# Two scan networks, two attention blocks and one ScalarE: dt as ln(1 + exp(x)), with the function tables loaded by the kernel

## The chip, the cores and the metric

The kernel runs on one NeuronCore of a Trainium2 chip. The metric is the device time of one execution in microseconds; a single run's time is that of this core. Five kinds of work run beside one another: TensorE matmuls (PE in the profile, its weight loads PEld), VectorE (DVE), ScalarE (ACT), GpSimd (POOL), and transfers that SyncE (SP) issues. Each engine runs its own instructions in program order and waits on semaphores for the others.

## The reference, cut to what matters

Four images of 56 x 56 tokens with 96 channels pass through four layers: a selective-scan block (L0), a second one with convolutions (L1), and two attention blocks with quantized feed-forward parts (L2, L3). Most of the work is in the selective scans. L0 and L1 each scan every image in four directions; this is one of them in L0:

```python
def selective_ssm(dtw, dtb, xw, A_log, D, seq):
    xz = jnp.einsum('bld,kd->blk', seq, xw)
    dt_raw = xz[..., :DT_RANK]
    b_ssm = xz[..., DT_RANK:DT_RANK + D_STATE]
    c_ssm = xz[..., DT_RANK + D_STATE:]
    dt = jax.nn.softplus(jnp.einsum('blr,dr->bld', dt_raw, dtw) + dtb)
    a = -jnp.exp(A_log)
    d_a = jnp.exp(dt[..., None] * a)
    d_b = dt[..., None] * b_ssm[:, :, None, :]
    def step(h, inp):
        da_t, db_t, x_t, c_t = inp
        h = da_t * h + db_t * x_t[..., None]
        y_t = jnp.einsum('bds,bs->bd', h, c_t)
        return (h, y_t)
    # ... jax.lax.scan over the 3136 tokens; 192 channels d, 16 states s
```

The step size dt is a softplus, ln(1 + exp(x)); the decay of each state is an exp of it. Around the scans the reference has a silu (of the gate z in L0 and L1, and after a convolution in L1) and a gelu (in the feed-forward part of L0). Those functions, and exp, run on ScalarE, which holds one set of function tables at a time.

## The kernel before: the parts that the change touches

A direction of an image is cut into 7 chunks of 448 tokens. A chunk is 8 rounds r = 0 to 7: two channel halves e times four groups q of states, with three scans (g = 0, 1, 2) a round. 2 layers x 4 images x 4 directions x 7 chunks make 224 chunks and 1792 rounds. While the rounds of one chunk run, the next chunk is prepared in pieces, one a round (the comments are added here):

```python
def step_size(self, ch, e, ps):                      # L476
    rows = slice(32, 32 + RANK[ch.l])
    self.nc.tensor.matmul(ps[:C], ch.par.wt[rows, C * e : C * e + C], ch.cf[rows], start=True, stop=True)
    return ps[:C]

def step_size_ahead(self, ch):                       # in round 1: half 1 into a "ps" bank, if one is free
    if self.held < BANKS:
        ch.pd.append(self.step_size(ch, 1, self.ps()[:, :CS]))

def softplus(self, ch):                              # in round 2: both halves
    for e in range(NE):
        if e == len(ch.pd):
            ch.pd.append(self.step_size(ch, e, self.pp()))
        dt = self.sp.tile([C, CS], F32, name="dtc")
        self.nc.scalar.activation(dt, ch.pd[e], AF.Softplus, bias=ch.par.dtb[:, e : e + 1])   # L492
        ch.dtc.append(dt)

def prepare(self, ch, follow, r):
    # ... r == 0: rows(follow), the projection from PSUM to SBUF
    elif r == 1:
        self.step_sizes(follow)                      # half 0 into the "pp" bank
        self.split(follow, 0)
    elif r == 2:
        self.softplus(follow)
        self.split(follow, 1)
    elif r == 3:
        self.times_u(follow, 0)                      # POOL: dt * u, L498
        for e in range(NE):
            self.park(follow.dtd, follow.dtc[e])     # to DRAM
    elif r == 4:
        self.times_u(follow, 1)
        # ... park and spread
```

The rounds themselves, and where work of the other layers is put between them:

```python
for n, (ch, e, q) in enumerate(rounds):
    # ...
    b, v, ahead = nxt
    for g in range(2 if ahead else 3):               # DVE, L659: v = du * b, b in PSUM
        nc.vector.tensor_tensor(v[:, g, TOKENS], ch.du[e][:, g], b, ALU.mult)
    self.prepare(ch, nexts.get(ch), r)
    self.half_round()
    self.spend((0.6, 0, 3.8, 0, 0, 0, 0, 0)[r], (0, 1.3, 0, 0, 0, 0, 1.3, 1.3)[r] + 1.3 * (r % NQ == 2))
    self.limit = ACT_LIMIT if r >= SOFTPLUS else 0.5 + 0.95 * 2 * (SOFTPLUS - r)
    yield "C", n, r                                  # slot C: steps of the other layers
    if more:
        nxt = begin(n + 1)                           # PE, L569: the next round's b
    if len(late) == 2:
        ended = late.pop(0)
        self.add_up(*ended)                          # PE: sums of the round two before, into y
    self.prepare_ahead(afters.get(ch), r)
    for g in range(NG):
        if g == 2:
            # ... keep_sums: ACT L721, Y <- y, after a round with q == 3
            yield "F", n, r                          # slot F: steps of the other layers
            if r == 1 and ch in nexts:
                self.step_size_ahead(nexts[ch])
        nc.vector.tensor_tensor_scan(v[:, g, way], da[g][:, way], v[:, g, way], 0.0, ALU.mult, ALU.add)  # L684
        # ... carry, then decay(n + 1, g): ACT L631, da = exp(na * dt), one of three
    nc.gpsimd.tensor_tensor(hc, v[:, :, TOKENS], ...)   # POOL L694: times C

def add_up(self, ch, e, q, hc):
    # ...
    for _ in range(int(max(0.0, WARM - self.work) / FILL + 0.5)):
        nc.tensor.matmul(self.y[:C], self.zeros, self.some, start=False, stop=False)   # L710, adds zeros
    # ... four matmuls of hc into y, L714
```

The steps of the other layers ("lanes": loading and the first projection, the middle with gelu, the convolution, the fusion, the attention) are generators. A step is started when its ScalarE and TensorE time fit into a running backlog (`room`, limits ACT_LIMIT 4.3 and PE_LIMIT 6.0) and when it holds no more than two "ps" banks with the others, one of which is lent away in rounds 0 and 1:

```python
held = sum(h[2] for h in self.live) - g[2] + new
fits = held <= self.banks - self.lend or new <= g[2] and held <= self.banks
if place[0] == self.slot and fits and self.room(act, pe):
    ...
```

Silu and gelu stand in such steps, as in the first projection:

```python
nc.scalar.activation(t[0], ps[0], AF.Silu, bias=b[:, 1:2])                  # L794
nc.scalar.activation(t[1][64:], ps[1][64:], AF.Silu, bias=b[64:, 2:3])
yield "F0 a.6"
```

No line of this kernel loads tables: the compiler puts a table load in front of an activation whose function the loaded set lacks. After the last scan the lanes that are left run alone, with more buffers (`late`).

Of the kernel before, what the change touches and what calls it, by code (L numbers as in the profile page):

```python
# [42 lines left out]
ACT_LIMIT, PE_LIMIT = 4.3, 6.0  # L43
SOFTPLUS = 2
BANKS, LATE_BANKS = 2, 4
# [5 lines left out]
ORDER = (((0, 0), (0, 1), (1, 0), (1, 1)), ((0, 1), (1, 0), (1, 1), (0, 0)))  # L51
WD = NE * 128 + NE * C + NE + NE * NQ * NG


# [109 lines left out]
class Net:  # L164
    def __init__(self, ctx, tc, aps, at, out):
        self.tc, self.nc, self.aps, self.at, self.out = tc, tc.nc, aps, at, out
        pool = lambda name, **kw: ctx.enter_context(tc.tile_pool(name=name, **kw))
        self.const = pool("const", bufs=1)
        self.big = pool("big", bufs=1)
        self.psum = pool("psum", bufs=1, space=bass.MemoryType.PSUM)  # L170
        self.dram = pool("dram", bufs=1, space=bass.MemoryType.DRAM)
        self.nw, self.depth, self.banks, self.ring = NW, DEPTH, BANKS, None
        self.setup()
        self.dg = None
        self.kept = (0, 0, 0)
        self.ready = set()
        self.held, self.lend, self.live, self.g = 0, 0, [], {}
        self.backlog, self.limit, self.paced = [0.0, 0.0], ACT_LIMIT, False
        self.work = 0.0
        self.U = [self.big.tile([C, L], F32, name=f"U{e}") for e in range(NE)]  # L180
        self.Y = [self.big.tile([C, L], F32, name=f"Y{e}") for e in range(NE)]
        self.wp = pool("work", bufs=2)
        self.scan_pool = ExitStack()
        self.sp = self.scan_pool.enter_context(tc.tile_pool(name="scan", bufs=2))
        self.pool = pool
        d = lambda name, *shape: [self.dram.tile(list(shape), F32, name=f"{name}{i}") for i in range(NB)]
        self.xd, self.xrd = d("x", C, L), d("xr", C, L)
        self.ud, self.zd, self.yd, self.md = d("u", DI, L), d("z", DI, L), d("y", DI, L), d("m", DI, L)

    def late(self):  # L190

        self.scan_pool.close()
        self.wp = self.pool("late", bufs=2)
        self.nw, self.depth, self.banks = LATE_NW, LATE_DEPTH, LATE_BANKS
        tags = (("ps", BANKS), ("da0", 1), ("da1", 1), ("da2", 1), ("pp", 1), ("b", 1), ("y", 1))
        self.ring = cycle([t for t in tags for _ in range(t[1])])
# [284 lines left out]

    def step_size_ahead(self, ch):

        if self.held < BANKS:
            ch.pd.append(self.step_size(ch, 1, self.ps()[:, :CS]))

    def softplus(self, ch):
        for e in range(NE):
            if e == len(ch.pd):
                ch.pd.append(self.step_size(ch, e, self.pp()))  # L490
            dt = self.sp.tile([C, CS], F32, name="dtc")
            self.nc.scalar.activation(dt, ch.pd[e], AF.Softplus, bias=ch.par.dtb[:, e : e + 1])  # L492
            ch.dtc.append(dt)

# [31 lines left out]
    def prepare(self, ch, follow, r):  # L526

        if r == 0:
            self.spread(ch.du, ch.dud[1], "du")
            self.spread(ch.dt, ch.dtd[1], "dt")  # L530
            self.fetch(ch, 3)
        if follow is None:
            return
        if r == 0:
            self.rows(follow)
        elif r == 1:
            self.step_sizes(follow)
# [46 lines left out]
    def scans(self):  # L584
# [23 lines left out]
        first, second = chunks[:2]  # L608
        self.held = 0
        self.parameters(first)  # L610
# [3 lines left out]
        for r in range(8):  # L614
            self.prepare(Step(), first, r) if r else self.rows(first)
        self.parameters(second)
        self.project_step(second, 0)
# [29 lines left out]

        nxt = begin(0)
        for g in range(NG):
            decay(0, g)  # L650
        late = []
        for n, (ch, e, q) in enumerate(rounds):
# [8 lines left out]
            self.half_round()  # L661
            self.spend((0.6, 0, 3.8, 0, 0, 0, 0, 0)[r], (0, 1.3, 0, 0, 0, 0, 1.3, 1.3)[r] + 1.3 * (r % NQ == 2))
            self.limit = ACT_LIMIT if r >= SOFTPLUS else 0.5 + 0.95 * 2 * (SOFTPLUS - r)
            yield "C", n, r
# [14 lines left out]
                    if r < SOFTPLUS:  # L679
                        self.limit -= 0.95  # L680
# [3 lines left out]
                nc.vector.tensor_tensor_scan(  # L684
# [16 lines left out]
    def add_up(self, ch, e, q, hc):  # L701

        nc = self.nc
        if q == 0:
# [77 lines left out]
    def project(self, l, i, xr, s):  # L782
# [11 lines left out]
        nc.scalar.activation(t[0], ps[0], AF.Silu, bias=b[:, 1:2])  # L794
        nc.scalar.activation(t[1][64:], ps[1][64:], AF.Silu, bias=b[64:, 2:3])
        yield "F0 a.6"
        nc.scalar.activation(t[1][:64], ps[1][:64], AF.Identity, bias=b[:64, 2:3])
# [50 lines left out]
    def window(self, d, rows, c):  # L848

        lo, hi = max(0, CR * c - 1), min(HS, CR * c + CR + 1)  # L850
        t = self.wp.tile([128, CR + 2, HS], F32, name="win", bufs=NWIN)[:rows]
        self.nc.sync.dma_start(
# [4 lines left out]
    def overlap(self, part, n, depth=9, ready=lambda c: True):  # L857
# [5 lines left out]
        while live or c < n:  # L863
# [4 lines left out]
            for g in list(live):  # L868
# [12 lines left out]
            self.held = sum(h[2] for h in self.live)  # L881
            yield
# [39 lines left out]
    def middle(self, i):  # L922
# [5 lines left out]
        def part(c):  # L928
# [18 lines left out]
            g.append(self.w())  # L947
            nc.scalar.activation(g[0], ps[0], AF.Gelu, bias=self.b1[:, :1])
            yield "C2 p2.6"
            for m in (1, 2):  # L950
# [3 lines left out]
            for m in (1, 2):  # L954
                g.append(self.w())
                nc.scalar.activation(g[m], ps[m], AF.Gelu, bias=self.b1[:, m : m + 1])
            yield "C1 p3.9"
            ps = self.ps()[:C, :CW]
# [14 lines left out]
        def convolve(c):  # L973
# [8 lines left out]
            t = self.w()  # L982
            nc.scalar.activation(t, ps, AF.Silu, bias=par("c128", "1conv_ba"))
            yield "C1 p2.2"
            ps = self.ps()
# [5 lines left out]
            for h in range(2):  # L991
                nc.scalar.activation(
                    t[:, h * CW // 2 : (h + 1) * CW // 2], o[h], AF.Silu, bias=par("c128", "1conv_bb")[:64]
                )
            yield "C0"
            nc.sync.dma_start(self.ud[i][128:, s], t)
# [234 lines left out]
def tile_net(ctx: ExitStack, tc: tile.TileContext, aps, at, out):  # L1231
# [5 lines left out]
    def alone(lanes):  # L1237
        net.slot, net.lend, net.paced = "C", 0, False
        while lanes:
# [10 lines left out]
    E = mybir.EngineType  # L1250
    with tc.manual_schedule(engines={E.PE, E.Activation, E.DVE, E.Pool}):
        lanes = []
        for slot, n, r in net.scans():
            p, u = divmod(n, rounds)
            net.slot, net.lend, net.paced = slot, int(r < 2), True
            if slot == "C" and u == 2 and p < 8:
# [29 lines left out]
```

## Time and profile before

| | us |
|---|---|
| time, median of 3 runs | 9209.74 (9199.88 to 9211.36) |
| profiled execution, span | 9209.2 |
| before the first scan | 111.4 |
| from the first scan to the end of the last | 8724.9 |
| after the last scan | 372.9 |
| DVE busy | 7881.9 (86%) |
| POOL busy | 7838.3 (85%) |
| PE busy | 7868.1 (85%) |
| ACT busy | 6148.3 (67%) |

"Busy" is the time in which an engine has at least one instruction running. In the list of groups a row gives line, engine, operation and tiles, the count behind an x, then after the bar the busy time of the group and the mean duration of one in ns, and after the second bar the idle time of that engine just before the group's instructions, with what ended it. In a view of waits each row is who waited <- for whom: us in total, times, longest us. In a timeline a row is start, duration, engine, line, operation, out<-in; the bracket tells how long the engine had been idle before it and what ended that.

### The profile page before, as it was taken

How to read it: one execution, taken by the hardware profiler on the slowest of the kernel's cores; microseconds unless marked ns; L12 is line 12 of the kernel's file. 1: busy time of each engine (PE TensorE's matmuls, PEld its weight loads, DVE VectorE, ACT ScalarE, POOL GpSimd, SP SyncE). 2: the span in 40 equal slices, each digit the busy share in tenths (PEclk: the TensorE clock that was granted, in tenths of full speed). 3: DMA queues.
4: the chain of work that ended last, by engine and by line, in shares of the span. 5: the costliest groups of instructions: out<-in, count | busy, mean ns of one | idle time of the engine just before them, and what ended most of it. 6: DMA issues, size and time to landing. Idle time of an engine off the chain costs nothing. (4 is left out here: it accounts for less than half of the span.)

```text
span 9209.2 us, 124390 instructions
## 1 busy us (share of the span) xinstructions
PE 7868.1 (85%) x35426; PEld 3036.5 (33%) x35426; DVE 7881.9 (86%) x10198; ACT 6148.3 (67%) x12259; POOL 7838.3 (85%) x4320
## 2 busy tenths in 40 slices
PE   7888888898888888988889888887888888987897
PEld 3333333333333333333333333333333333333344
DVE  5999999899998999989988997899888898888941
ACT  5777677676777677766776655577656776566645
POOL 5998989989898989889888997899888998888941
PEclk9899989989899988999888998888888888887986
DMA  5776676667666676767666775566755567655721
GB/s 151 176 179 169 166 171 164 157 153 177 162 168 157 157 181 161 169 150 177 162 148 152 168 170 136 136 153 160 171 138 143 141 164 172 147 138 134 168 77 39
DMA packets 951352, 1418.11 MB, mean 154 GB/s; under 512 B 176578, under 2 KB 943812, under 8 KB 949796
## 3 DMA queue, kind: packets, MB, share of 16 engines
q1 hardware_dynamic: 949888, 1408.37, 63.5%
q8 instruction: 278, 4.55, 0.2%
q14 instruction: 414, 3.39, 0.1%
q10 hardware_dynamic: 772, 1.80, 0.1%
HBM read 1141.42 MB, written 268.14 MB: 153 GB/s over the span
## 5 line engine op out<-in xcount | busy, mean ns | idle before, releaser
L684 DVE TENSOR_TENSOR_SCAN v<-da,v 128x449 f32<-128x449 f32 (+1 forms) x5376 | 5484.4, 1072 | 244.6 <-ACT da L631 111.0
L694 POOL TENSOR_TENSOR hc<-v,cb 128x1344 f32<-128x1344 f32 x1792 | 5168.0, 2885 | 573.5 <-DVE v L684 257.2
L631 ACT ACTIVATE da<-dt,na 128x448 f32<-128x448 f32 x5376 | 3392.8, 635 | 1690.3 <-DVE v L684 1650.9
L659 DVE TENSOR_TENSOR v<-du,b 128x448 f32<-128x448 f32 x4172 | 2342.3, 609 | 663.0 <-PE b L569 532.4
L714 PE MATMUL y<-hc,four 128*32 128x448 f32 x14336 | 1913.8, 609 | 0.0
L710 PE MATMUL y<-w,zeros 128*96 128x448 bf16 x7084 | 1716.6, 380 | 0.0
L639 POOL TENSOR_TENSOR v<-du,cb 128x448 f32<-128x448 f32 x1204 | 1373.7, 1141 | 79.0 <-DMA cb<-cd 41.6
L710 PEld LDWEIGHTS <-zeros 128*96 128x96 bf16 x7084 | 918.5, 130 | 1049.4 <-issue 639.9
L569 PE MATMUL b<-cf,sel 128*128 128x448 bf16 x1792 | 708.3, 395 | 350.9 <-DVE v L659 350.1
L761 POOL TENSOR_TENSOR rs<-rs,power 112x4 f32<-112x4 f32 x252 | 254.2, 1010 | 546.9 <-ACT rs L760 361.6
L427 PE MATMUL pp<-U,wd 96*128 96x448 f32 x896 | 674.5, 840 | 14.3 <-DMA U<-u 14.3
L721 ACT COPY Y<-y 96x448 f32<-96x448 f32 x448 | 341.3, 762 | 468.8 <-PE y L714 468.4
L841 PE MATMUL ps<-win,dg 64*64 64x220 f32 (+10 forms) x1962 | 568.4, 491 | 55.3 <-ACT dtc L492 47.0
L714 PEld LDWEIGHTS y<-hc,four 128*32 128x32 f32 x14336 | 295.3, 113 | 951.0 <-issue 649.1
L498 POOL TENSOR_TENSOR duc<-dtc,U 96x448 f32<-96x448 f32 x448 | 559.6, 1249 | 2.5 <-ACT dtc L492 2.5
L708 PE MATMUL y<-Y,ident 96*96 96x448 f32 x672 | 543.4, 898 | 11.4 <-ACT carry L688 8.9
L631 ACT ACT_TABLE_LOAD x385 | 494.0, 1283 | 15.1 <-DMA dt<-dd 8.3
L582 POOL TENSOR_TENSOR cf<-cf 64x448 f32<-64x448 f32 x448 | 417.7, 932 | 38.1 <-ACT cf L466 3.0
L569 PEld LDWEIGHTS <-sel 128*128 128x128 bf16 x1792 | 195.4, 109 | 741.4 <-issue 737.9
L688 ACT COPY carry<-v 128x3 f32<-128x3 f32 x1536 | 295.7, 193 | 172.1 <-DVE v L684 169.6
L765 PE MATMUL ps<-ident,rs 112*96 112x112 f32 x1752 | 267.7, 308 | 158.3 <-POOL rs L761 87.7
L841 PEld LDWEIGHTS ps<-win,dg 64*64 64x64 f32 (+2 forms) x1962 | 236.8, 169 | 423.7 <-issue 317.2
(414 smaller groups left out, 6457.5 us busy)
## 6 DMA issues: line engine op xcount, KB each, us to landing
cb<-cd SPq DMA_DIRECT2D x3584, 112.0 KB, 4.1
dt<-dd SPq DMA_DIRECT2D x1792, 168.0 KB, 4.4
du<-dd SPq DMA_DIRECT2D x1792, 168.0 KB, 4.2
dd<-dtc SPq DMA_DIRECT2D x448, 168.0 KB, 2.0
dd<-duc SPq DMA_DIRECT2D x448, 168.0 KB, 2.0
U<-u SPq DMA_DIRECT2D x112, 168.0 KB, 4.5
z<-w SPq DMA_DIRECT2D x56, 224.0 KB, 3.8
u<-w SPq DMA_DIRECT2D x56, 224.0 KB, 3.2
```

Of the source, the lines that this page charges most:

```text
L427: self.nc.tensor.matmul(ch.ps.rearrange("p (a b) -> p a b", b=HS), ch.par.wx[:, e], self.in_order(self.U[e], ch.orient, ch.c * CS, CS), st ...
L498: self.nc.gpsimd.tensor_tensor(du.rearrange("p (a b) -> p a b", b=HS), ch.dtc[e].rearrange("p (a b) -> p a b", b=HS), self.in_order(self.U ...
L569: self.nc.tensor.matmul(ps, self.sel[:, q], self.upper(ch.cf), start=True, stop=True)
L631: nc.scalar.activation(da[g][:, TOKENS], ch.dt[e][:, g], AF.Exp, scale=ch.par.na[:, e, q, g : g + 1])
L639: nc.gpsimd.tensor_tensor(v[:, 2, TOKENS], ch.du[e][:, 2], ch.cb[q][:, 1], ALU.mult)
L659: nc.vector.tensor_tensor(v[:, g, TOKENS], ch.du[e][:, g], b, ALU.mult)
L684: nc.vector.tensor_tensor_scan(v[:, g, way], da[g][:, way], v[:, g, way], 0.0, ALU.mult, ALU.add)
L694: nc.gpsimd.tensor_tensor(hc, v[:, :, TOKENS], ch.cb[q][:, 0].unsqueeze(1).to_broadcast([128, NG, CS]), ALU.mult)
L708: nc.tensor.matmul(o, w, self.in_order(a, ch.orient, ch.c * CS, CS), start=True, stop=False)
L710: nc.tensor.matmul(self.y[:C], self.zeros, self.some, start=False, stop=False)
L714: nc.tensor.matmul(self.y[32 * n : 32 * n + 32], self.four, hc[:, g], start=n == 3, stop=n == 3 or q == NQ - 1,)
L841: self.nc.tensor.matmul(o[:, a - r0 : e - r0, x0:x1], diag[:, tap], win[:, a + dy - lo : e + dy - lo, x0 + dx : x1 + dx], start=n == 0, st ...
```

## The change

dt is computed as ln(1 + exp(x)) by two activations, Exp and then Ln with a bias of 1, in place of one Softplus. One set of tables holds both exp and ln (set 6). The kernel loads it itself: once in front of the scans, and again behind every silu and gelu, so that neither the decays nor dt need another set. dt of half 0 is made in round 2 and of half 1 in round 3. With that go the devices that made room for the old round 2: the lent bank, the lower ScalarE limit in rounds 0 and 1, the second projection ahead into a "ps" bank (it now goes into "pp" in round 2). Two smaller things go along: no filler matmuls ahead of the sums that end a half (q == 3), and more window buffers after the last scan.

```diff
+EXP_AND_LN = 6
...
-        self.nw, self.depth, self.banks = LATE_NW, LATE_DEPTH, LATE_BANKS
+        self.nw, self.nwin, self.depth, self.banks = LATE_NW, LATE_DEPTH, LATE_DEPTH, LATE_BANKS
...
-    def step_size_ahead(self, ch):
-
-        if self.held < BANKS:
-            ch.pd.append(self.step_size(ch, 1, self.ps()[:, :CS]))
-
-    def softplus(self, ch):
-        for e in range(NE):
-            if e == len(ch.pd):
-                ch.pd.append(self.step_size(ch, e, self.pp()))
-            dt = self.sp.tile([C, CS], F32, name="dtc")
-            self.nc.scalar.activation(dt, ch.pd[e], AF.Softplus, bias=ch.par.dtb[:, e : e + 1])
-            ch.dtc.append(dt)
+    def softplus(self, ch, e):
+        dt = self.sp.tile([C, CS], F32, name="dtc")
+        self.nc.scalar.activation(dt, ch.pd[e], AF.Exp, bias=ch.par.dtb[:, e : e + 1])
+        self.nc.scalar.activation(dt, dt, AF.Ln, bias=1.0)
+        ch.dtc.append(dt)
...
         elif r == 2:
-            self.softplus(follow)
+            self.softplus(follow, 0)
             self.split(follow, 1)
         elif r == 3:
+            self.softplus(follow, 1)
             self.times_u(follow, 0)
-            for e in range(NE):
-                self.park(follow.dtd, follow.dtc[e])
+            self.park(follow.dtd, follow.dtc[0])
         elif r == 4:
             self.times_u(follow, 1)
+            self.park(follow.dtd, follow.dtc[1])
...
-            self.spend((0.6, 0, 3.8, 0, 0, 0, 0, 0)[r], (0, 1.3, 0, 0, 0, 0, 1.3, 1.3)[r] + 1.3 * (r % NQ == 2))
-            self.limit = ACT_LIMIT if r >= SOFTPLUS else 0.5 + 0.95 * 2 * (SOFTPLUS - r)
+            self.spend((0.7, 0, 1.3, 1.3, 0, 0, 0, 0)[r], (0, 1.3, 1.3, 0, 0, 0, 1.3, 1.3)[r] + 1.3 * (r % NQ == 2))
...
-                    if r == 1 and ch in nexts:
-                        self.step_size_ahead(nexts[ch])
+                    if r == 2 and ch in nexts:
+                        nexts[ch].pd.append(self.step_size(nexts[ch], 1, self.pp()))
...
-        for _ in range(int(max(0.0, WARM - self.work) / FILL + 0.5)):
+        for _ in range(int(max(0.0, WARM - self.work) / FILL + 0.5) if q < NQ - 1 else 0):
...
+    def exp_and_ln(self):
+        scalar = self.nc.scalar
+        scalar.add_instruction(
+            mybir.InstLoadActFuncSet(
+                name=self.nc.get_next_instruction_name(), engine=mybir.EngineType.Activation, act_func_set_id=EXP_AND_LN
+            )
+        )
...
         nc.scalar.activation(t[1][64:], ps[1][64:], AF.Silu, bias=b[64:, 2:3])
+        self.exp_and_ln()
         yield "F0 a.6"
...                  # likewise behind the gelus (two places) and the silus of the convolution (two places)
-                fits = held <= self.banks - self.lend or new <= g[2] and held <= self.banks
-                if place[0] == self.slot and fits and self.room(act, pe):
+                if place[0] == self.slot and held <= self.banks and self.room(act, pe):
...
-        return not self.paced or (act == 0 or a + act <= self.limit) and (pe == 0 or p + pe <= PE_LIMIT)
+        return not self.paced or (act == 0 or a + act <= ACT_LIMIT) and (pe == 0 or p + pe <= PE_LIMIT)
...
     with tc.manual_schedule(engines={E.PE, E.Activation, E.DVE, E.Pool}):
+        net.exp_and_ln()
```

More of the change, by code (lines that the diff above doesn't have):

```diff
@@ L43 @@
 ACT_LIMIT, PE_LIMIT = 4.3, 6.0
-SOFTPLUS = 2
 BANKS, LATE_BANKS = 2, 4
@@ L171, in __init__ @@
         self.dram = pool("dram", bufs=1, space=bass.MemoryType.DRAM)
-        self.nw, self.depth, self.banks, self.ring = NW, DEPTH, BANKS, None
+        self.nw, self.nwin, self.depth, self.banks, self.ring = NW, NWIN, DEPTH, BANKS, None
         self.setup()
@@ L176, in __init__ @@
         self.ready = set()
-        self.held, self.lend, self.live, self.g = 0, 0, [], {}
-        self.backlog, self.limit, self.paced = [0.0, 0.0], ACT_LIMIT, False
+        self.live, self.g = [], {}
+        self.backlog, self.paced = [0.0, 0.0], False
         self.work = 0.0
@@ L608, in scans @@
         first, second = chunks[:2]
-        self.held = 0
         self.parameters(first)
@@ L615, in scans @@
             self.prepare(Step(), first, r) if r else self.rows(first)
+            if r == 2:
+                first.pd.append(self.step_size(first, 1, self.pp()))
         self.parameters(second)
@@ L678, in scans @@
                         self.keep_sums(*ended[:3])
-                    if r < SOFTPLUS:
-                        self.limit -= 0.95
                     yield "F", n, r
-                    if r == 1 and ch in nexts:
-                        self.step_size_ahead(nexts[ch])
+                    if r == 2 and ch in nexts:
+                        nexts[ch].pd.append(self.step_size(nexts[ch], 1, self.pp()))
                 nc.vector.tensor_tensor_scan(
@@ L795, in project @@
         nc.scalar.activation(t[1][64:], ps[1][64:], AF.Silu, bias=b[64:, 2:3])
+        self.exp_and_ln()
         yield "F0 a.6"
@@ L850, in window @@
         lo, hi = max(0, CR * c - 1), min(HS, CR * c + CR + 1)
-        t = self.wp.tile([128, CR + 2, HS], F32, name="win", bufs=NWIN)[:rows]
+        t = self.wp.tile([128, CR + 2, HS], F32, name="win", bufs=self.nwin)[:rows]
         self.nc.sync.dma_start(
@@ L880, in overlap @@
                         self.live.remove(g)
-            self.held = sum(h[2] for h in self.live)
             yield
@@ L948, in part @@
             nc.scalar.activation(g[0], ps[0], AF.Gelu, bias=self.b1[:, :1])
+            self.exp_and_ln()
             yield "C2 p2.6"
@@ L956, in part @@
                 nc.scalar.activation(g[m], ps[m], AF.Gelu, bias=self.b1[:, m : m + 1])
+            self.exp_and_ln()
             yield "C1 p3.9"
@@ L983, in convolve @@
             nc.scalar.activation(t, ps, AF.Silu, bias=par("c128", "1conv_ba"))
+            self.exp_and_ln()
             yield "C1 p2.2"
@@ L994, in convolve @@
                 )
+            self.exp_and_ln()
             yield "C0"
@@ L1237, in alone @@
     def alone(lanes):
-        net.slot, net.lend, net.paced = "C", 0, False
+        net.slot, net.paced = "C", False
         while lanes:
@@ L1254, in tile_net @@
             p, u = divmod(n, rounds)
-            net.slot, net.lend, net.paced = slot, int(r < 2), True
+            net.slot, net.paced = slot, True
             if slot == "C" and u == 2 and p < 8:
```

## The prediction

> **What bounds the kernel now.** I read the page's groups first, for who is busy:
>
> ```profile
> L684 DVE TENSOR_TENSOR_SCAN v<-da,v 128x449 f32<-128x449 f32 (+1 forms) x5376 | 5484.4, 1072 | 244.6 <-ACT da L631 111.0
> L694 POOL TENSOR_TENSOR hc<-v,cb 128x1344 f32<-128x1344 f32 x1792 | 5168.0, 2885 | 573.5 <-DVE v L684 257.2
> L631 ACT ACTIVATE da<-dt,na 128x448 f32<-128x448 f32 x5376 | 3392.8, 635 | 1690.3 <-DVE v L684 1650.9
> L659 DVE TENSOR_TENSOR v<-du,b 128x448 f32<-128x448 f32 x4172 | 2342.3, 609 | 663.0 <-PE b L569 532.4
> L631 ACT ACT_TABLE_LOAD x385 | 494.0, 1283 | 15.1 <-DMA dt<-dd 8.3
> ```
>
> ScalarE idles 1651 us waiting for the scans, so on average it has time. VectorE has little: three scans (3 x about 1.0 us) and two or three products fill most of a round, and its largest wait is the 532 us for b, a PE matmul. GpSimd has about the same busy time. The 1792 rounds take 8724.9 us, 4.87 us each.
>
> An average hides where in a chunk the time is lost, so I sorted the trace's VectorE records by the round in which they start, taking a round from its first scan to the next round's first scan. Over all 224 chunks the mean lengths of rounds 0 to 7 are 4.41, 4.37, 6.49, 5.14, 4.38, 4.81, 4.58 and 4.76 us, and VectorE idles 60, 46, 314, 167, 32, 72, 88 and 136 us in them, 915 us in all. Round 2 alone has a third of it. It is the round of the softplus. The timeline of one such place:
>
> ```profile
> 3926.83 0.64 ACT L631 ACTIVATE da<-dt,na 128x448 f32<-128x448 f32 x1
> 3927.48 1.28 ACT L492 ACT_TABLE_LOAD   x1
> ...
> 3928.78 0.63 ACT L492 ACTIVATE dtc<-pp,wd 96x448 f32<-96x448 f32 x1
> ...
> 3929.31 0.62 ACT L492 ACTIVATE dtc<-ps,wd 96x448 f32<-96x448 f32 x1
> ...
> 3929.95 1.28 ACT L631 ACT_TABLE_LOAD   x1
> ...
> 3929.98 3.33 PE L841 MATMUL ps<-win,dg 128*128 128x448 f32 x4 [3.16 <-ACT dtc L492]
> ...
> 3933.10 0.58 PE L569 MATMUL b<-cf,sel 128*128 128x448 bf16 x1
> ...
> 3933.72 1.69 DVE L659 TENSOR_TENSOR v<-du,b 128x448 f32<-128x448 f32 x3 [5.06 <-PE b L569]
> ```
>
> The reader is to see a chain: softplus is in another set of tables, so ScalarE loads, makes both halves and loads back, from 3927.48 to 3931.23, 3.75 us in one piece. The second half was projected into a "ps" bank. The next lane step (here a convolution, L841) wants a bank, and PE, which keeps its order, stands still 3.16 us until ScalarE has read it. The b of the next round stands behind that step, and VectorE waits 5.06 us. For each VectorE wait in round 2 that b ended, I took the longest wait of PE just before it: 225 of round 2's 314 us (103 places) lead back to dtc, L492.
>
> **What the Trainium skill says.** "ScalarE: Activation LUTs", section "Table sets: the hidden batching unit": `natural_log_exp_and_others` holds exp and ln, and the cheap functions stand in every set. So the kernel's copies, squares and identities should add no load. Its section "What ACT_TABLE_LOAD costs" gives 1283 ns and about 1380 ns of drain for every switch. The trace has the 1283 ns in all 776 loads; the drain does not show: before a load ScalarE idles 18 ns in the median, after it 12 ns. I price a load at 1.28 us. "ScalarE activation tables: per-element evaluation and per-set limits", section "What a function is on this engine", says that the cost doesn't depend on the table. The trace agrees: softplus 619 to 630 ns, exp 635 ns, silu 634 ns.
>
> **The change part by part.**
>
> *Loads.* Before: 385 (L631) + 224 (L492) + 51 (L794) + 4 x 28 (gelu and convolution) + 4 in the setup = 776. After: silu and gelu have 56 groups in the projection, 56 with gelu and 56 in the convolution, each with one load there and one back: 336, and some six in front, about 342. That is 434 fewer x 1.283 = 557 us less on ScalarE. The pair of loads around each silu or gelu stays.
>
> *Activations.* 448 Softplus become 448 Exp of the same length. 448 Ln are added, SBUF to SBUF with a pointer bias; like L1079, with the same size and operands, which took 662 ns: 448 x 0.66 = 296 us. ScalarE's busy time goes from 6148 to about 6148 - 557 + 296 = 5890 us. None of this is on the path by itself; ScalarE keeps over a third of the span idle.
>
> *The burst.* This is what counts. In round 2 ScalarE has Exp and Ln, 1.3 us, in place of 3.75 us, and the same in round 3. Three decays (1.9 us) and the two carries (0.2 us each, partly beside them) leave about 1.8 us of a 4.1 us round, so 1.3 us fits. No dt holds a "ps" bank any more. The 225 us should go nearly whole. Of round 3's 167 us, 56 us are waits for the carry copy (L646) that came late behind the burst; I take 45. Some of the other waits of round 2 for ScalarE and for rs on GpSimd go as well, about 25 us. Sum: 295 us.
>
> *Rounds 0 and 1.* The lanes get both banks and the whole limit there. Those rounds, now nearly without waits (60 and 46 us), will see more of the lanes' matmuls, up to some 40 us of new waits. Against that the lanes are spread more evenly over rounds 3 to 7, whose waits for b and da (105 us in round 7, 52 us in round 6) should shrink by as much. I count zero.
>
> *Fillers.* The sums that end a half fall in rounds 1 and 5, so those rounds' fillers go: about 3.7 and 5.1 of them on average by the trace's count, some 1990 of the 7084. Elsewhere the new TensorE charge of 1.3 in round 2 drops some four more a chunk. PE busy falls by roughly 700 to 1000 us (380 ns each as shown). In the timeline above, ScalarE had waited 3.35 us for y just before the burst, with three fillers at 3923.58 ahead of y's last sums. Y <- y waits 468 us in all. I give 30 us for a y that comes earlier.
>
> *What takes part of it back.* GpSimd works 7760 of the 8725 us of the scans. A round that ends sooner leaves it less idle time, and it is in lockstep through the v and hc buffers. I take off a tenth: 325 - 30 = about 295 us.
>
> *After the last scan,* 372.9 us. Five of the seven fusion parts of the last image are still to do then, and the sixth and seventh start late, behind three windows. With six windows they overlap, but PE is busy 40 of each 40 us there until 8960 us, so only the last part's lonely stretch (8960 to 9001 us) can shrink: some 15 us. Lanes that come further in the scans leave less: 10 us. *Before the first scan* redundant loads behind seven silus add at most 9 us, mostly beside PE: +3 us.
>
> Sum: 9210 - 295 - 25 + 3 = about 8893; the lanes' lighter load on ScalarE in all other rounds is not in it, and I lean a little to the fast side for it: **8870 us**, 3.7% less.
>
> **The rivals.**
>
> *GpSimd becomes the bound.* For it: 33.5 to 36.2 us busy a chunk, VectorE 34.4 to 35.5, against chunks of 36.9 to 41.0 us; in round 3 most of the waits besides the carry are for buffers or for GpSimd (57 us that the profile puts to "issue", 25 us for rs). Against it: even in the passes of the fusion and attention, at 41.0 us a chunk, there are 4.8 us between GpSimd's work and the round. If it held, half the gain would be lost: about 9030 us.
>
> *The wait moves to the new "pp" projection.* Half 1 is now projected in round 2 behind half 0's Exp, and PE waits there for ScalarE; if ScalarE is behind with lanes, b of round 4 is late. For it: where half 1 went through "pp" before (14 of 224 chunks), PE waited 42 us in all, 3 us each. Against it: there the Exp stood behind a load, and PE comes to it only in the last third of the round. If it held: 9000 us.
>
> *The gain is larger.* If rounds 2 and 3 fell to the 0.3 us of idle time that the others have on average, 481 us would become about 145, and the lanes' lead would shorten the end: 8790 us, with freed PE time 8700 us.
>
> *A colder array.* Fewer fillers might lower the granted clock (0.887 now, 0.857 in the last pass of the scans). "TensorE: Matmul & The Clock Gate", section "What's actually happening", describes a gate that opens with recent activity; the profile shows 0.56 to 0.66 in the late stretch from 9000 us on, where PE has gaps. Lane matmuls would take longer. PE is not on the path where it has slack, so I give it 20 to 60 us at most.
>
> **Range and chances.** The firm part is the 225 us with a known cause; the rest is give and take of some 100 us either way. The range is 8690 to 9020 us. Faster by over 2% means under 9025.5 us; the first two rivals together would have to hold for less: faster 0.88, within 2% 0.11, slower 0.01.
>
> **What would show it.** Right: about 342 loads, none at L492's successor; Ln at 0.6 to 0.7 us; ScalarE busy near 5890 us; VectorE idle in round 2 under 100 us of 224 chunks, and no PE wait for dtc of more than a few us; VectorE's busy time unchanged at 7880 us. Wrong: if rounds 4 to 7 or 0 and 1 grow by what round 2 loses; if GpSimd is busy all through rounds 2 to 4 and VectorE waits for hc or v; or if loads appear in front of decays, because the compiler does not know of the kernel's own.

## The result, and the profile after

The kernel after takes 8997.89 us (median of 4 runs, 8973.38 to 9007.72) against 9210.55 us: a ratio of 0.9766, with a 95% interval of 0.9743 to 0.9789. That is inside the predicted range and faster by over 2%, but the gain is 213 us where 340 were forecast.

The groups of the page after; the columns are as before (line numbers have moved: L682 is the scan, L660 the product, L568 makes b, L489 is the Exp of dt):

```profile
L692 POOL TENSOR_TENSOR hc<-v,cb 128x1344 f32<-128x1344 f32 x1792 | 5165.0, 2884 | 382.5 <-DVE v L682 225.8
L660 DVE TENSOR_TENSOR v<-du,b 128x448 f32<-128x448 f32 x4172 | 2341.5, 608 | 583.3 <-PE b L568 450.4
L719 ACT COPY Y<-y 96x448 f32<-96x448 f32 x448 | 339.7, 758 | 291.4 <-PE y L712 288.2
L489 ACT ACTIVATE dtc<-pp,wd 96x448 f32<-96x448 f32 x448 | 279.5, 624 | 291.4 <-PE pp L480 289.3
```

VectorE and GpSimd do the same work in a shorter span. The row of the scans in the longer list names three causes of its waits; here it is before and after:

```profile
L684 DVE TENSOR_TENSOR_SCAN v<-da,v 128x449 f32<-128x449 f32 (+1 forms) x5376 | 5484.4, 1072 | 244.6 <-ACT da L631 111.0 <-ACT v L646 70.2 <-POOL v L639 57.0
L682 DVE TENSOR_TENSOR_SCAN v<-da,v 128x449 f32<-128x449 f32 (+1 forms) x5376 | 5478.2, 1071 | 143.0 <-POOL v L639 56.4 <-ACT da L631 55.6 <-ACT v L646 27.0
```

The scans wait 83 us for ScalarE (decays, L631, and carry copies, L646) where they waited 181 us. The wait for b, as the profile names it, has gone down by 82 us only, from 532 to 450. That is a difference of two moves: in round 2 it fell from 277 to 35 us, in the other seven rounds it rose from 255 to 415 us.

ScalarE in a round 2 of the kernel after (its timeline; start, duration, then the instruction):

```profile
3016.67 0.64 ACT L631 ACTIVATE da<-dt,na 128x448 f32<-128x448 f32 x1
3017.24 0.62 ACT L489 ACTIVATE dtc<-pp,wd 96x448 f32<-96x448 f32 x1
3017.90 0.58 ACT L490 ACTIVATE dtc<-dtc 96x448 f32<-96x448 f32 x1
3018.38 0.62 ACT L631 ACTIVATE da<-dt,na 128x448 f32<-128x448 f32 x1
```

From the end of one decay to the start of the next there are now 1.1 us for one half of dt (the other half comes in round 3), where both halves with their two loads had taken 3.75 us in one piece.

VectorE's idle time, sorted by round as in the prediction (my sums over the 224 chunks from each trace, in us; "scans" is the time from the first scan to the end of the last, "tail" what comes after it). The variants are those of the experiments below:

| | r0 | r1 | r2 | r3 | r4 | r5 | r6 | r7 | scans | tail |
|---|---|---|---|---|---|---|---|---|---|---|
| before | 60 | 46 | 314 | 167 | 32 | 72 | 88 | 136 | 8725 | 373 |
| after | 98 | 104 | 80 | 93 | 42 | 74 | 34 | 199 | 8524 | 331 |
| before, one set of tables | 59 | 53 | 215 | 106 | 29 | 79 | 91 | 136 | 8569 | 359 |
| before, no fillers there | 73 | 54 | 273 | 147 | 27 | 66 | 65 | 173 | 8684 | 374 |
| after, lanes out of r0, r1 | 96 | 38 | 53 | 148 | 68 | 81 | 49 | 177 | 8501 | 372 |
| after, Softplus | 122 | 113 | 71 | 212 | 79 | 70 | 65 | 189 | 8740 | 369 |
| before, projection moved | 36 | 36 | 283 | 145 | 28 | 52 | 65 | 59 | 8501 | 344 |
| after, projection moved | 67 | 82 | 60 | 134 | 49 | 57 | 49 | 75 | 8361 | 332 |

Each row is one profiled execution. That of the kernel after took 8973 us, the shortest of its four (median 8998), that with the lanes out of rounds 0 and 1 took 8989 us, the longest of its four (median 8944). So the rows tell where the waits are; what a change is worth is read from the medians.

Rounds 2 and 3 gave 308 us. The other six took 117 us back: 96 in rounds 0 and 1, 63 in round 7 and 12 in rounds 4 and 5, less 54 that round 6 gave. The question for the experiments was which part of the change gave, and what took.

### The profile page after: what moved, and what is told of

It reads as the page before. It is cut to its first block, busy times and chain, and to the rows that moved or that the text cites. A ratio compares the mean times of both kernels' runs of the same rounds, so it can differ in the third digit from the quotient of the medians.

```text
span 8971.7 us, 119757 instructions
## 1 busy us (share of the span) xinstructions
PE 7571.7 (84%) x33219; PEld 2802.4 (31%) x33219; DVE 7868.1 (88%) x10198; ACT 5815.9 (65%) x12281; POOL 7829.5 (87%) x4320
## 5 line engine op out<-in xcount | busy, mean ns | idle before, releaser
L682 DVE TENSOR_TENSOR_SCAN v<-da,v 128x449 f32<-128x449 f32 (+1 forms) x5376 | 5478.2, 1071 | 143.0 <-POOL v L639 56.4
L631 ACT ACTIVATE da<-dt,na 128x448 f32<-128x448 f32 x5376 | 3392.9, 634 | 1546.4 <-DVE v L682 1485.0
L660 DVE TENSOR_TENSOR v<-du,b 128x448 f32<-128x448 f32 x4172 | 2341.5, 608 | 583.3 <-PE b L568 450.4
L712 PE MATMUL y<-hc,four 128*32 128x448 f32 x14336 | 1988.7, 631 | 2.7 <-POOL hc L692 2.5
L708 PE MATMUL y<-w,zeros 128*96 128x448 bf16 x4877 | 1236.4, 391 | 0.0
L568 PE MATMUL b<-cf,sel 128*128 128x448 bf16 x1792 | 719.0, 401 | 604.0 <-DVE v L660 602.8
L708 PEld LDWEIGHTS <-zeros 128*96 128x96 bf16 x4877 | 652.0, 134 | 778.7 <-issue 515.5
L428 PE MATMUL pp<-U,wd 96*128 96x448 f32 x896 | 694.2, 863 | 19.1 <-DMA U<-u 19.0
L849 PE MATMUL ps<-win,dg 64*64 64x220 f32 (+10 forms) x1962 | 546.6, 474 | 19.1 <-DMA win<-x 16.3
L480 PE MATMUL pp<-cf,wd 12*96 12x448 f32 (+1 forms) x896 | 498.0, 638 | 0.4 <-ACT dtc L489 0.2
L489 ACT ACTIVATE dtc<-pp,wd 96x448 f32<-96x448 f32 x448 | 279.5, 624 | 291.4 <-PE pp L480 289.3
L568 PEld LDWEIGHTS <-sel 128*128 128x128 bf16 x1792 | 194.3, 108 | 747.5 <-issue 743.4
```

What stands on the lines that cost most here:

```text
L428: self.nc.tensor.matmul(ch.ps.rearrange("p (a b) -> p a b", b=HS), ch.par.wx[:, e], self.in_order(self.U[e], ch.orient, ch.c * CS, CS), st ...
L568: self.nc.tensor.matmul(ps, self.sel[:, q], self.upper(ch.cf), start=True, stop=True)
L631: nc.scalar.activation(da[g][:, TOKENS], ch.dt[e][:, g], AF.Exp, scale=ch.par.na[:, e, q, g : g + 1])
L712: nc.tensor.matmul(self.y[32 * n : 32 * n + 32], self.four, hc[:, g], start=n == 3, stop=n == 3 or q == NQ - 1,)
L849: self.nc.tensor.matmul(o[:, a - r0 : e - r0, x0:x1], diag[:, tap], win[:, a + dy - lo : e + dy - lo, x0 + dx : x1 + dx], start=n == 0, st ...
```

## The experiments

Theory A: ScalarE's piece in round 2 was too long, and its length, made up mostly of table loads, is what counts. Theory B: what counts is that dt no longer holds a "ps" bank and goes half by half. For what was taken back there were three theories: the fillers that were left out and the clock (C), the lanes that moved into rounds 0 and 1 (D), and too many matmuls between two b's in round 7 (F).

All times are medians; each ratio is against the kernel before on the same chip.

| run | us | ratio | 95% interval |
|---|---|---|---|
| b_oneset | 9049.93 | 0.9839 | 0.9823 to 0.9855 |
| b_fill | 9147.86 | 0.9938 | 0.9918 to 0.9958 |
| b_onesetfill | 9026.48 | 0.9816 | 0.9798 to 0.9835 |
| a_fill | 8977.83 | 0.9768 | 0.9752 to 0.9785 |
| a_softplus | 9208.86 | 1.0017 | 1.0005 to 1.0030 |
| a_compiler | 9497.87 | 1.0342 | 1.0310 to 1.0375 |
| a_thin | 8943.53 | 0.9734 | 0.9711 to 0.9756 |
| a_nosplit | 8951.03 | 0.9739 | 0.9716 to 0.9761 |
| a_proj | 8826.36 | 0.9601 | 0.9579 to 0.9623 |
| b_proj | 8959.65 | 0.9750 | 0.9730 to 0.9770 |
| a_thinproj | 8848.76 | 0.9617 | 0.9602 to 0.9631 |
| a_projown | 8854.16 | 0.9632 | 0.9614 to 0.9650 |

**One set of tables alone (b_oneset).** On the kernel before; its own loads stand in front of the scans and behind each silu and gelu, as in the change.

```diff
-            self.nc.scalar.activation(dt, ch.pd[e], AF.Softplus, bias=ch.par.dtb[:, e : e + 1])
+            self.nc.scalar.activation(dt, ch.pd[e], AF.Exp, bias=ch.par.dtb[:, e : e + 1])
+            self.nc.scalar.activation(dt, dt, AF.Ln, bias=1.0)
```

> The kernel before with only the function changed: Exp then Ln, the set with both loaded by the kernel itself, but both halves still in round 2 and the second still in a lent ps bank. Theory A (the length of the piece of ScalarE work counts): the piece shrinks from 3.75 to about 2.4 us against some 1.8 us of room, so about two thirds of the 225 us of round 2 go: 9030 to 9090 us. Theory B (the ps bank and the order count, not the loads): under 40 us gained, above 9170 us.

Measured: 9050 us, as theory A had it. Round 2 loses 99 us of idle time and round 3 61 us; no other round changes by over 7 us. Nothing is paid back here, with the bank still lent and the lanes still held out of rounds 0 and 1. From the list of groups, VectorE's product, and the kernel's own loads:

```profile
L661 DVE TENSOR_TENSOR v<-du,b 128x448 f32<-128x448 f32 x4172 | 2344.3, 610 | 565.6 <-PE b L570 448.0 <-issue 63.7 <-DMA du<-dd 20.4
L747 ACT ACT_TABLE_LOAD x163 | 209.1, 1283 | 2.9
```

This alone already brings the wait for b to 448 us, the same sum as in the kernel after, but not in the same places: 180 us of it still stand in round 2, against 35 us there. PE still waits for dt in the lent bank: 182 us over all rows of its waits for dtc, against 264 us in the kernel before.

**The schedule alone (a_softplus).** The kernel after, half by half and without a bank, but with Softplus.

```diff
-        self.nc.scalar.activation(dt, ch.pd[e], AF.Exp, bias=ch.par.dtb[:, e : e + 1])
-        self.nc.scalar.activation(dt, dt, AF.Ln, bias=1.0)
+        self.nc.scalar.activation(dt, ch.pd[e], AF.Softplus, bias=ch.par.dtb[:, e : e + 1])
...
-            self.spend((0.7, 0, 1.3, 1.3, 0, 0, 0, 0)[r], ...
+            self.spend((0.7, 0, 3.2, 3.2, 0, 0, 0, 0)[r], ...
```

> The kernel after, one half per round and no ps bank, but with the one Softplus (charged 3.2 us of ScalarE time each) and so a load before and after it: 3.2 us in one piece in round 2 and again in round 3. Theory A (the length of the piece counts): the waits of rounds 2 and 3 come back, 9080 to 9200 us. Theory B (not holding a ps bank is what counts): 8990 to 9040 us.

Measured: 9209 us, the time of the kernel before and just outside the range that theory A gave. As a cause of the gain by itself theory B falls: without the change of tables, the rest of the change is worth nothing. As the route of the wait in round 2 the bank is confirmed: PE's wait for dtc falls from 264 us to 3 us with the loads still there, and the wait for b in round 2 to 35 us, as in the kernel after. The waits have another face. The b of round 3 is no longer late (round 2 has 71 us), but the decays and carries behind the pieces are, as this group of the scans shows:

```profile
L680 DVE TENSOR_TENSOR_SCAN v<-da,v 128x449 f32<-128x449 f32 (+1 forms) x5376 | 5483.1, 1072 | 271.6 <-ACT v L645 137.5 <-ACT da L630 69.9 <-POOL v L638 57.8
L630 ACT ACT_TABLE_LOAD x608 | 780.1, 1283 | 18.7 <-DMA dt<-dd 8.1
L489 ACT ACT_TABLE_LOAD x447 | 573.5, 1283 | 7.9
```

Half by half, each dt has a pair of loads of its own: 1222 loads in all against 776 in the kernel before, and ScalarE is busy 6696 us against 6148 us. So this run doesn't tell what the order would be worth with as many loads as before. Together with the common set it is worth something: from b_oneset to the kernel after, round 2 goes from 215 to 80 us and the ratio from 0.9839 to 0.9766.

**The kernel's own loads (a_compiler).** The kernel after with every load of its own taken out.

```diff
-        self.exp_and_ln()
```

> The kernel after without any load of its own, so that the compiler picks the sets. It should go to a set with exp for every Exp and to one with ln for every Ln: four loads a chunk, 3.7 us in one piece in rounds 2 and 3, some 1060 loads in all. Theory A: 9150 to 9350 us, slower than or like the kernel before. Theory B: below 9050 us.

Measured: 9498 us, more than theory A's upper end and 3.4% slower than the kernel before. The compiler loads one set in front of each Ln and another in front of the decay behind it, two for every half; in all 1225 loads (I had counted too few, 1060):

```profile
L681 DVE TENSOR_TENSOR_SCAN v<-da,v 128x449 f32<-128x449 f32 (+1 forms) x5376 | 5486.3, 1072 | 529.1 <-ACT v L646 342.0 <-ACT da L631 133.3 <-POOL v L639 46.9
L490 ACT ACT_TABLE_LOAD x448 | 574.8, 1283 | 7.9
```

The Trainium skill ("ScalarE: Activation LUTs", "Table sets: the hidden batching unit") counts one load for ln followed by exp. Here that holds only where the kernel asks for the common set; left to the compiler there was one load for each change from exp to ln and one for each change back. ScalarE is busy 6929 us, 73% of the span, and yet the scans wait 475 us for it. That the length of the piece does this, and not the sum, fits the 27% of the span in which ScalarE is idle; as both grew in this run, it is not shown by it alone.

**The fillers (b_fill, a_fill, b_onesetfill).** The first leaves them out in the kernel before, the second puts them back into the kernel after, the third leaves them out of b_oneset. The edit is this line, or its opposite:

```diff
-        for _ in range(int(max(0.0, WARM - self.work) / FILL + 0.5)):
+        for _ in range(int(max(0.0, WARM - self.work) / FILL + 0.5) if q < NQ - 1 else 0):
```

> The kernel before with only the fillers ahead of the last sums of each half left out. Theory A (fillers delay y and b there): 9160 to 9200 us, ScalarE's wait for y falls by a third. Theory C (fillers hold the TensorE clock up, and their loss is what ate a part of the gain): granted clock 0.86 to 0.87 in place of 0.887 and slower, 9230 to 9290 us.

> The kernel after with these fillers put back. Theory A: 9000 to 9040 us, as the sums come later in rounds 1 and 5. Theory C: granted clock back at 0.88 to 0.89, matmuls 3% shorter, waits in rounds 7, 0 and 1 shrink, 8900 to 8960 us.

> The kernel before with two parts of the change together: one set of tables for exp and ln (both halves still in round 2, the second in a lent ps bank), and the fillers ahead of a half's last sums left out. The two alone gave 0.984 and 0.994. Theory I (they add up, and making one half per round without a bank adds nothing to them): 8970 to 9010 us, like the kernel after. Theory J (they take away the same waits, and one half per round brings the rest): 9035 to 9070 us.

Measured: 0.9938 on the kernel before, a little better than theory A had it, nothing on the kernel after (0.9768 against 0.9766, between the ranges of both theories), and 0.9816 with the tables, again between the two: the intervals of b_oneset (from 0.9823) and of this one (to 0.9835) overlap a little. Theory C falls as a cause of the missing gain. The clock did go down, 0.848 in b_fill and 0.859 in the kernel after against 0.887 before and 0.897 in a_fill, but a_fill with the higher clock is no faster. Two waits follow the fillers. One is ScalarE's wait for y; the filler group and ScalarE's copy of y, first of a_fill, then of the kernel after:

```profile
L708 PE MATMUL y<-w,zeros 128*96 128x448 bf16 x6649 | 1622.5, 381 | 0.0
L719 ACT COPY Y<-y 96x448 f32<-96x448 f32 x448 | 341.3, 762 | 449.0 <-PE y L712 447.4
```

```profile
L708 PE MATMUL y<-w,zeros 128*96 128x448 bf16 x4877 | 1236.4, 391 | 0.0
L719 ACT COPY Y<-y 96x448 f32<-96x448 f32 x448 | 339.7, 758 | 291.4 <-PE y L712 288.2
```

ScalarE waits 159 us more for y with the fillers, and the time is the same. In the kernel before, whose burst began right behind that copy, leaving them out was worth 57 us (0.62% of 9205); that it is the earlier y which brings this is likely, but the fillers' own time on PE went with it.

The other is VectorE's wait in round 7. By the same sums it is longer without these fillers in all three pairs: 136 and 173 us (before, b_fill), 136 and 182 us (b_oneset, b_onesetfill), 171 and 199 us (a_fill, after). So 28 to 46 us of the 63 that round 7 took back go with the fillers; whether through the lower clock was not tried. Round 6 is 11 to 36 us shorter in the same pairs, so the loss hardly shows in the sum.

**Lanes out of rounds 0 and 1 (a_thin).** The lent bank and the lower limit of the kernel before, put back into the kernel after.

```diff
-            net.slot, net.paced = slot, True
+            net.slot, net.lend, net.paced = slot, int(r < 2), True
...
-                if place[0] == self.slot and held <= self.banks and self.room(act, pe):
+                fits = held <= self.banks - self.lend or new <= g[2] and held <= self.banks
+                if place[0] == self.slot and fits and self.room(act, pe):
...
+            self.limit = ACT_LIMIT if r >= 2 else 0.5 + 0.95 * 2 * (2 - r)
```

> The kernel after, but lanes are kept out of rounds 0 and 1 as before (one bank lent, the lower ScalarE limit). Theory D (the gain was eaten where lanes moved into rounds 0 and 1): VectorE idle in these two rounds falls from 202 us to about 110 us and the time to 8900 to 8960 us. Theory E (the lanes' matmuls cost the same wherever they stand): the waits move to rounds 3 to 7, 8980 to 9060 us.

Measured: 8944 us, in theory D's range, but the ratio's interval overlaps that of the kernel after. Rounds 0 and 1 have 134 us, not 110. Round 1 gives 66 us, round 0 stays (98 and 96 us), and rounds 3 and 4 take 81; the tail grows from 331 to 372 us, probably because lanes held back are left over at the end. So theory D has the place right for round 1 alone and at most a small part of the sum; most of what the lanes cost they cost wherever they stand (theory E). With the projection moved (a_thinproj, below) they gave nothing either.

**GpSimd (a_nosplit).** The subtraction in `split` is left out, so the low part of B is missing and its values are wrong by it.

```diff
-        self.nc.gpsimd.tensor_tensor(x, x, self.upper(x), ALU.subtract)
+        return x
```

> The kernel after without GpSimd's subtraction on cf (448 instructions, 418 us; this leaves out the low part of B and its values are wrong by it). Theory G (GpSimd has become the bound): 8650 to 8800 us. Theory H (PE's order and b are the bound, GpSimd only in round 3): VectorE idle in round 3 falls by half, 8900 to 8970 us.

Measured: 8951 us. GpSimd has 419 us less to do (7410 us against 7830), and the kernel gains at most some tens of us; the intervals overlap. GpSimd is not the bound (theory G falls). The time is in theory H's range, but round 3, which was to lose half, goes from 93 to 88 us only: that part of H falls as well.

**The projection (a_proj, b_proj).** Here is a round 7 of the kernel after in the timeline:

```profile
7841.12 2.00 PE L428 MATMUL pp<-U,wd 96*128 96x448 f32 x2
...
7842.93 1.68 PE L1053 MATMUL ps<-w,cen 128*128 128x448 f32 x2
...
7844.54 1.18 PE L1054 MATMUL ps<-w,neg 64*128 64x448 f32 x2
...
7845.65 0.37 PE L568 MATMUL b<-cf,sel 128*128 128x448 bf16 x1
...
7846.06 1.15 DVE L660 TENSOR_TENSOR v<-du,b 128x448 f32<-128x448 f32 x2 [3.49 <-PE b L568]
```

No engine has kept PE here; PE is at work without a break from the projection of the chunk after next (L428) through four matmuls of a lane, and b comes behind them. Ahead of the projection in round 6 stand the start of the next y and its sums. Both kernels do this; I moved the first half of the projection from round 6 to 5 and left the second in round 7, with the inputs it needs a round earlier:

```diff
-            elif r == 5:
+            elif r == 4:
                 self.inputs(far)
-            elif r > 5:
-                self.project_step(far, r - 6)
+            elif r in (5, 7):
+                self.project_step(far, r // 7)
...
-            self.spend(..., (0, 1.3, 1.3, 0, 0, 0, 1.3, 1.3)[r] + 1.3 * (r % NQ == 2))
+            self.spend(..., (0, 1.3, 1.3, 0, 0, 1.3, 0, 1.3)[r] + 1.3 * (r % NQ == 2))
```

(In the kernel before the first list has a zero in the place of round 2.)

> The kernel after with the projection of the chunk after next in rounds 5 and 7 in place of 6 and 7, its inputs a round earlier. Theory F (PE has too much between b of round 7 and b of round 0: the start of y, a projection, the sums and lanes): VectorE idle in round 7 falls from 199 to about 120 us, 8900 to 8960 us. Theory E (the matmuls cost the same wherever they stand): round 5 takes what round 7 loses, 8980 to 9020 us.

> The kernel before with only the projection of the chunk after next in rounds 5 and 7 in place of 6 and 7. Theory K (the wait in round 7 was there before the change, and the move takes it away in the same measure): round 7 from 136 to about 70 us, 9050 to 9130 us. Theory L (it became long only through the change, which sends lanes there): 9170 to 9210 us.

Measured: 8826 us on the kernel after and 8960 us on the kernel before, better than both theories' ranges. VectorE's product in the list of groups, of a_proj and then of b_proj:

```profile
L660 DVE TENSOR_TENSOR v<-du,b 128x448 f32<-128x448 f32 x4172 | 2336.7, 607 | 451.3 <-PE b L568 289.2 <-issue 65.2 <-DMA du<-dd 33.9
```

```profile
L659 DVE TENSOR_TENSOR v<-du,b 128x448 f32<-128x448 f32 x4172 | 2339.2, 608 | 550.9 <-PE b L569 415.8 <-issue 58.3 <-DMA du<-dd 26.1
```

Theory F holds. In the kernel after round 7 loses 124 us, rounds 0 and 1 53 us; round 3 takes 41 of it back. In the kernel before round 7 loses 77 us. So this wait was there before the change (theory K, in which I had the worth of the move too low) and the change made it longer by 63 us; the move takes away both. a_proj is faster than both kernels of this case, by 4.0% and, from the two ratios, by about 1.7% against the kernel after.

In the kernel before the move does more than that. ScalarE's wait for y falls from 468 us nearly to that of b_fill (275 us), in part because the projection now counts as work in round 5 and so takes fillers out of it (1149 to 506):

```profile
L721 ACT COPY Y<-y 96x448 f32<-96x448 f32 x448 | 340.8, 761 | 292.3 <-PE y L714 290.3
```

Rounds 2, 3 and 6 give 31, 22 and 23 us there, and gave 41, 20 and 23 us in b_fill. So a part of b_proj's 240 us, at most some 57 by this estimate, is probably what leaving out fillers brings too; no run shows it. The kernel after has next to no fillers in round 5 (21), which fits the smaller worth of the move in it: 0.9766 x 0.9750 = 0.952 would be the two changes multiplied, 0.9601 was measured.

**Two tries to better it (a_thinproj, a_projown).** The first is a_thin and a_proj together. The second changes GpSimd's share of the products:

```diff
-OWN = (3, 4, 6)
+OWN = (2, 3, 4)
```

> The kernel after with the projection in rounds 5 and 7, and with lanes kept out of rounds 0 and 1. Theory D (lanes in rounds 0 and 1 cost what the change gives elsewhere): 8770 to 8810 us. Theory E (they cost the same in any round, and held back they lengthen the stretch after the last scan): 8820 to 8880 us.

> The kernel after with the projection in rounds 5 and 7, and with GpSimd's share of the products left out in rounds 2, 3 and 4 in place of 3, 4 and 6 (chunks of L0 and of the first image of L1 alone), so that GpSimd has less to do ahead of round 3's wait. Theory G (GpSimd's backlog makes the 134 us of round 3): 8750 to 8800 us. Theory H (it moves the wait to rounds 6 and 7): 8810 to 8870 us.

Measured: 8849 and 8854 us; neither is faster than a_proj (theories E and H). Round 3 has 128 us in a_projown against 134: its wait isn't made by GpSimd's products of rounds 2 and 3. The profile puts 65 of a_proj's 134 us there to "issue" and most of the rest to GpSimd. The timeline shows the matmul behind these names; here is the longest such wait of a_proj:

```profile
5318.66 1.75 PE L1060 MATMUL ps<-w,neg 128*64 128x448 f32 x2
...
5320.35 1.75 PE L1061 MATMUL ps<-w,cen 64*64 64x448 f32 x2
...
5322.03 3.25 PE L849 MATMUL ps<-win,dg 96*96 96x440 f32 x4
...
5325.07 0.58 PE L568 MATMUL b<-cf,sel 128*128 128x448 bf16 x1
...
5325.74 1.68 DVE L660 TENSOR_TENSOR v<-du,b 128x448 f32<-128x448 f32 x3 [6.67 <-issue]
```

The product starts 0.09 us after b's end. That holds for 65 places of round 3 in a_proj, 119 of its 134 us: each starts 93 to 95 ns after the end of a b, and PE was at work all the time, for 90 us of it on lanes. In the kernel after it is 89 of 93 us. So round 3 is the wait of round 7 once more: too many matmuls of lanes ahead of b. That fits what a_nosplit and a_projown did to it, which is little, and a_thin, which sent lanes there and made round 3 longer (148 us). No run took lanes away from this place.

## Why the prediction was right or wrong, step by step

- **The burst: right.** The step gave 250 us for round 2 and 45 us for round 3, 295 us in all. The traces show 234 and 74, 308 us. b_oneset shows that the tables by themselves bring 160 of it in those rounds, and a_softplus that the rest of the change without them brings nothing to the time; the other 148 us came where both were together.
- **Loads and activations: right in kind, one price too high.** 350 loads against about 342, none of them in front of a copy or a square. One sign of being wrong did appear, loads in front of decays, but in the first four chunks only. Ln took 577 ns, not 662; I had priced it by an activation that reads its bias from a tile. ScalarE is busy 5816 us, not 5890.
- **"Rounds 0 and 1 ... I count zero": this step failed.** All rounds but 2 and 3 together should have stayed as they were; they wait 117 us more. With 117 us put at that place, the forecast for the scans (295 - 117 = 178 us) would have been near the measured 201 us. The expected shrinking of round 7 was its weakest part: I took its 105 us for something that lanes spread more evenly would relieve, where PE simply had too much in that stretch. a_proj and b_proj show that. Of the extra 63 us, 28 to 46 went with the fillers; the rest fits the lanes (PE works 1.20 us a round on them in round 7 against 1.00 before by my sums) but no run shows it. Of the 96 us in rounds 0 and 1, a_thin shows that lanes in round 1 make some 66; round 0's 38 us did not go with the lanes, and with the projection moved 31 us of them went, so they fit a queue of PE that reaches over from round 7.
- **The lean to 8870 us: not borne out.** The sum was 8893 us; the 23 us that I took off for a lighter load on ScalarE in the other rounds went the wrong way. The range held because it was wide.
- **The 30 us for an earlier y: wrong for this kernel.** Fewer fillers are worth 57 us while the burst stands behind the copy and nothing after it (b_fill, a_fill). PE busy fell by 296 us, not 700 to 1000: 2207 fillers fewer are 480 us by their group, and the other matmuls got longer.
- **GpSimd takes a tenth back: not shown.** GpSimd is not the bound, as the first rival would have had it: 419 us less work for it brought some tens of us at most (a_nosplit). What I read as a sign for it in round 3, 57 us of "issue" and 25 us for rs, were waits for b: of round 3's 167 us, 95 end 93 to 95 ns after a b, with PE at work throughout.
- **The rival of the "pp" projection: wrong.** PE waits 0.2 us in all for the dt that frees that bank; ScalarE waits for PE there (289 us) and has the time. That the time came out near this rival's 9000 us is chance.
- **The larger gain: not in this change.** Its 8790 us are nearly what a_proj reaches, by a move in a place that the change doesn't touch.
- **The colder array:** the clock fell to 0.859, and the 20 to 60 us that I gave it do not show in the sum of a_fill. Its round 7 is 28 us shorter, but rounds 0 to 2 and 6 are 35 us longer.
- **Before and after the scans:** +6 us against +3, and 42 us off the tail against 25. With the windows put back alone I have no run; a_thin, which has the same windows but lanes further behind, has a tail of 372 us, and b_proj, with the old windows, one of 344 us; so it is likely the lanes' lead that shortens it.

## What to carry to other kernels

An engine that is two thirds busy can still set the time, by the longest piece of work that it does without a break while the others' queues stand in order behind it: sort the idle time of the busiest engine by its place in the loop before looking at sums. Each switch of tables cost two loads here, one there and one back, at the place where they were least wanted; one set for all functions of the loop removed them, but only when the kernel asked for that set. When such a piece goes, the work that had been kept away from it moves, and the next place with too much work between two steps of the path takes part of the gain: look for that place at once. And do not stop at the name that a profile gives a wait: in round 3 it said GpSimd and "issue" where a matmul had ended 0.09 us before.

## What the runs showed of the hardware that I had not expected

- A load takes 1283 ns, whichever function it is for, and leaves no other mark: the 448 loads in front of Ln in a_compiler have 7.9 us of idle time before them in all, and over all 1225 loads of that run ScalarE idles 12 ns (median) behind one.
- Ln with a constant bias, from SBUF to SBUF, takes 577 ns for 448 elements; an activation of the same size whose bias stands in a tile takes 663 ns (L1089).
- The load in front of the scans did not hold from the start: 17 loads of the compiler in front of decays and Ln stand between 113 and 239 us, in the first four chunks, and none after that. Why the compiler puts them there was not tried.
- The granted clock followed the fillers (0.897 with them, 0.859 without in the kernel after) and the time of that kernel did not.
